# A planned order drawn up anew: other due times, and a longer landing time of scatter-adds in the table of costs

## Chip, core and metric

One core of a Trainium2 chip runs the whole kernel in one launch. The metric is the time of that launch in device microseconds (us). The engines are TensorE (PE, with its weight load PEld), VectorE (DVE), ScalarE (ACT), GpSimd (POOL) and SyncE (SP). SP issues most of the DMAs, ACT some of them, and POOL the indirect ones (gather and scatter).

## What is computed

The input x has the shape (32, 56, 56, 128): 32 images of 3136 tokens with 128 channels. Two layers follow each other.

```python
# layer 0
x = x + binary_conv3x3(LN(x))          # batch-norm over all images, then sign
t = t + moe(LN(t))                     # router, best 2 of 8 experts, each 128 -> 128
# layer 1
y = LN(x)
a = sigmoid((y @ Wa1) * (y @ Wa2)); b = sigmoid((y @ Wb1) * (y @ Wb2))
z = einsum("bikc,bkjc->bijc", a, b)    # 16 channels
x = x + sigmoid(y @ Wg) * (LN(z) @ Wz + bz)
t = t + ffn(LN(t))
def ffn(y):                            # each image by itself
    probs = softmax(y @ gate_w.T, axis=tokens)              # 64 experts
    vals, idx = top_k(probs, 8 tokens of each expert)
    pooled = sum over the 8 of vals * y[idx]                # one row per expert
    o = gelu(pooled @ W1 + b1) @ W2 + b2                    # 128 -> 512 -> 128
    out[idx] += vals * o                                    # scatter-add, 8 rows per expert
```

The last part matters most here: each image and each of the 64 experts give eight rows that are added to eight tokens of the output.

## The kernel before

**Tiles and stages.** The work is cut into 16 pairs of images, and each pair into 7 units of 896 tokens (a tile of 128 partitions x 7 x 128). A first pass over all 112 units gathers the statistics of the batch-norm (L494, L1843). Then the pairs flow through the stages: fetch and sign, convolution (L639) and its way back (L581), the mixture of experts (gate rows loaded by SP into gb, the product gb x xT on DVE in L833, the expert matmuls in L838, the sum in L850), the triangle mixing (L896, the z product in L982, L1095, L1117), and the logits of the 64 experts (L1168). In the steady state a pair comes out every 193 us, by the trace.

**The end of a pair.** `top8` searches the best eight tokens (L1195, L1199) on DVE, the softmax follows, and POOL gathers the tokens' rows with eight indirect DMAs (L1228). `pool_rows` adds them up weighted (L1246, L1248) and turns them on PE (tr_p, L1257).

**Late experts.** The 64 expert networks run in 16 groups of four. Each group runs twice, since its weights are needed for the images that are ready early and again for the last ones. `late_experts(False, g)` serves the first 13 pairs (images 0 to 25): weights on SP (L1418 the first, L1420 the second, L1465 the pooled rows, L1497 the bias), then ph (L1485), trh (L1509), gelu, po (L1531), and for each of the four experts a spreading product ps_eo (L1557), which lays an expert's output rows out for the eight tokens of every image. DVE scales them into a buffer eo (L1575, once for each of two lots: images 0 to 13, 112 rows, and 14 to 25, 96 rows), and POOL scatter-adds the buffer to the output (L1588). That makes 64 pairs of eo writes and 128 scatter-adds. There are four eo buffers (NEO, L73). Within a lot each scatter-add waits until the one before it has landed, since both may add to one token; between the lots POOL sets a byte in a memset (L1322), which keeps them apart. `late_experts(True, g)` ("alone") serves the last three pairs: its weights go to places of tiles that are done with (yT, the frames, lines, a_bd, gb, x, xT), the bias is added in L1517, and the results go to a buffer in memory (o_last_d, L1546).

**The last rows.** `last_sums` lays out for each of the last three pairs which expert adds to which token (store near_d in L1646, loads in L1650 and L1662, DVE in L1656, L1672 and L1680) and gathers the output rows concerned (L1696, 24 on POOL). `last_load` (L1721) brings the alone results back, in two parts: experts 0 to 47 and experts 48 to 63. `last_out_rows` multiplies (PE, L1744), adds (DVE, L1758), and POOL writes the rows out (L1775, 24 of them: 18 in the first part, 6 in the second).

**What sets the order.** Nothing is issued as the code is read. Each operation is recorded in an object of class `Order` (L92): engine, a duration in ns, for some a landing time, the tiles and keys that it reads and writes, and a rank. When all are recorded, `Order.run` (L166) plays the program through with these durations: on each engine it takes, of the operations that are ready, the one of lowest rank that can have its tiles; a tile comes free when its last user has ended. For a scatter-add that end is that of POOL plus the landing time:

```python
ends[k] = end + land
...
free[t.args[1]][slot[t]] = ends[k] + self.LAG[e]
```

The order found so is then emitted, and each engine keeps it on the chip whatever the real times are. The numbers in the table are costs for this planning only.

The rank is a due time in ticks. `TICK` (L38 to L69) has a row for each stage, with one number for each unit, batch, half or group; `PERIOD` is 14 ticks per pair:

```python
def at(p, tick):
    if tick > 19.3:
        tick = 19.3 + SHRINK.get(p, 1.0) * (tick - 19.3)
    return p * PERIOD + tick
```

`SHRINK` is 0.94 for the last pair. The 16 groups of `late_first` count from pair 13, those of `late_alone` and all rows of `last_` from pair 15. So a due time moves an operation on every engine that it uses, its SP and POOL issues too, as far as its inputs and buffers allow.

Of the kernel before, what the change touches and what calls it, by code (L numbers as in the profile page):

```python
# [35 lines left out]
PERIOD = 14  # L36

TICK = {  # L38
    "fetch": (-2.04, 1.47, 6.43, -9.37, 9.91, 4.03, 12.95),
    "sign": (0.13, 1.29, 1.62, 6.55, 7.92, 10.76, 8.15),  # L40
    "conv": (2.01, 2.39, 6.91, 8.17, 10.9, 11.53, 13.69),
    "conv_back": (3.38, 3.29, 7.78, 8.94, 11.21, 12.17, 14.95),
    "moe_turn": (6.33, 4.64, 9.97, 10.08, 12.86, 12.68, 15.65),
    "moe_gates": (6.55, 7.48, 10.31, 10.2, 14.16, 14, 16.57),
    "moe_experts": (10.08, 7.97, 10.43, 10.33, 15.78, 14.17, 16.99),
    "moe_add0": (10.49, 11.31, 14.68, 13.22, 16.78, 17.09, 19.52),
    "moe_add1": (10.74, 10.2, 14.52, 11.86, 17.39, 15.02, 19.11),
    "tri_turn": (16.98, 17.15, 20.55, 19.2, 19.88, 19.01, 20.48),
    "moe_stats": (4.49, 9.18, 12.45, 15.62),
    "moe_route": (6.46, 10.13, 12.89, 15.74),  # L50
    "tri_stats": (15.38, 15.09, 17.71, 20.29),
    "tri_b": (20.72, 21.13),
    "tri_a": (22.16, 21.48),
    "tri_z": (22.52,),
    "tri_out": (23.16, 22.58, 25.59, 25.25, 26.33, 28.87, 29.55),
    "gate_stats": (23.66, 26.32, 27, 31.44),
    "gate_turn": (25.56, 26.72, 27.08, 28.41, 30.53, 32.72, 31.77),
    "gate_logits": (26.34, 28.28, 30.27, 30.73, 30.88, 33.55, 33.56, 33.61),
    "clear": (33.78,),
    "top8": (36.48,),  # L60
    "pool_rows": (40.09,),
    "late_first": (28.35, 29.89, 30.07, 31.23, 36.99, 38.58, 41.48, 41.79, 42.49, 44.88, 49.22,
        50.09, 53.49, 56.47, 57.12, 73.25),
    "late_alone": (48.05, 52.09, 68.6, 70.4, 66.27, 52.32, 44.78, 60.5, 76.55, 41.92, 67.99,
        67.49, 84.16, 107, 76.56, 68.5),
    "last_sums": (54.98, 70.08, 51.49),
    "last_load": (79.71, 120.93),
    "last_rows": (102.26, 131.4, 121.75, 140.19, 135, 143.81),
}  # L69

AHEAD_CHAIN = 2
# [214 lines left out]
def kernel(ctx: ExitStack, tc: tile.TileContext, a: dict, out: bass.AP):  # L286
# [116 lines left out]
    def apart(ins, k):  # L403

        for other in range(len(LOTS)):
            if other != k:
                tc.declare_no_dep(ins, group=f"lot{other}", reason="the lots' tokens differ")
        tc.add_to_no_dep_group(f"lot{k}", ins)


    with ExitStack() as c2:
# [32 lines left out]
        def new(tag, shape, name, dtype=F32):  # L444
            return op.tile(pools.get(tag, work), tag, shape, dtype, name)
# [4 lines left out]
        def bank(name):  # L450
            return new("ps", [128, 512], name)
# [867 lines left out]
        def part_lots(lot):  # L1319

            if pool_lot["last"] not in (None, lot):
                nc.gpsimd.memset(between, 0.0)  # L1322
            pool_lot["last"] = lot
# [33 lines left out]
        def late_experts(alone, g):  # L1357
# [74 lines left out]
            for j in range(NE):  # L1432
                h = homes[j]
                if h == "p":
                    for k, of in ((0, first_w), (1, second_w)):
                        _, key, (keys, base) = of[j]

                        @op("SP", 360, r=[open_place(keys, base)], w=[key], land=868)
                        def _(j=j, k=k):
                            load_w(j, k)  # L1440
                elif h == "g" and alone:
                    @op("SP", 720, w=[first_w[j][1]], land=1736)
                    def _(j=j):
                        load_w(j, 0)
                        load_w(j, 1)
                else:
                    @op("SP", 360, w=[first_w[j][1]], land=868)
                    def _(j=j):
                        load_w(j, 0)

                    if alone:
                        load_second(j)
# [9 lines left out]
            else:  # L1462
# [17 lines left out]
            @op(  # L1480
                "PE", 1000, r=[key for _, key, _ in first_w] + [(side1, "t")], w=[ph, ("ph", name)]
            )
            def _():
                for j in range(NE):
                    nc.tensor.matmul(  # L1485
                        ph.ap[32 * j : 32 * j + 32, :], lhsT=tok()[:, j].rearrange("c p i -> c (p i)"),
                        rhs=first_w[j][0](),
                        start=True, stop=True,
                    )
# [37 lines left out]
            @op("PE", 1100, r=[hG] + [key for _, key, _ in second_w], w=[po])  # L1527
            def _():
                for k in range(HID4):
                    for j in range(NE):  # L1530
                        nc.tensor.matmul(  # L1531
                            po.ap[32 * j : 32 * j + 32, :C],
                            lhsT=hG.ap[:, k, 32 * j : 32 * j + 32], rhs=second_w[j][0]()[:, k * C : (k + 1) * C],
                            start=(k == 0), stop=(k == HID4 - 1),
                        )
# [14 lines left out]
            for j in () if alone else range(NE):  # L1550
                ps_e = bank(f"ps_eo_{name}_{j}")

                @op("PE", 2 * 222, r=[(side2, "o")], w=[ps_e])
                def _(q=B * j, ps_e=ps_e):
                    for k, (i0, i1) in enumerate(LOTS[:2]):
                        rows = (i1 - i0) * K1
                        nc.tensor.matmul(  # L1557
                            ps_e.ap[:rows, k * C : (k + 1) * C],
                            lhsT=spread[q : q + B, k, :rows], rhs=side2.ap[q : q + B, 5, :],
                            start=True, stop=True,  # L1560
                        )

                eo = new("eo", [128, 2, C], f"eo_{name}_{j}")

                for lot in range(2):
                    i0, i1 = LOTS[lot]
                    rows = (i1 - i0) * K1
                    e = g * NE + j

                    @op(  # L1570
                        "DVE", 230, r=[ps_e] + [("picked", p) for p in range(i0 // 2, i1 // 2)],
                        w=[(eo, lot)],
                    )
                    def _(eo=eo, lot=lot, rows=rows, e=e, ps_e=ps_e, k=lot):
                        nc.vector.tensor_scalar(  # L1575
                            eo.ap[:rows, lot, :], ps_e.ap[:rows, k * C : (k + 1) * C],
                            gains[lot][:rows, e : e + 1], None, ALU.mult,
                        )

                    @op(  # L1580
                        "POOL", 2000, land=4200,
                        r=[(eo, lot)] + [("out", p, u) for p in range(i0 // 2, i1 // 2)
                                         for u in range(NU)][: None if e == 0 else 0],
                        w=[("lot", lot)],
                    )
                    def _(eo=eo, lot=lot, rows=rows, e=e):
                        part_lots(lot)
                        ins = nc.gpsimd.indirect_dma_start(  # L1588
                            out=tokens_out,
                            out_offset=bass.IndirectOffsetOnAxis(  # L1590
                                ap=picked[lot][:rows, e : e + 1], axis=0
                            ),
                            in_=eo.ap[:rows, lot, :], in_offset=None, compute_op=ALU.add,
                        ).ins

                        for before_ in last_out.get(lot, stored[lot]):
                            tc.add_manual_dep(ins, before_, sync, reason="adds to the same tokens")
                        apart(ins, lot)
                        last_out[lot] = [ins.name]
# [598 lines left out]
```

## Time and profile before

| what | value |
|---|---|
| time, median of 3 runs | 3759.09 us (3744.3 to 3762.89) |
| time of the profiled execution | 3770.89 us |
| its span; mean granted clock of TensorE | 3769.1 us; 0.958 |
| PE busy / PEld busy | 3440.6 us (91%) / 2811.6 us (75%) |
| DVE / ACT / POOL busy | 3223.4 (86%) / 2371.0 (63%) / 464.6 us (12%) |
| DMA | 834.19 MB, 221 GB/s in the mean |
| first and last eo write (L1575) | 3180.3 and 3664.9 us |
| first and last scatter-add issued (L1588) | 3180.9 and 3688.7 us; 128, mean 1693 ns of POOL each |
| search of the last pair (L1195); its first and last gather (L1228) | 3604.09; 3613.99 and 3622.85 us |
| first issue of the last rows (L1775) | 3724.2 us |

The profile is of one execution. A share of busy time is a mean over the whole span, and the busy tenths by slices (40 slices of 94 us) show that the run has two halves of unequal kind:

```profile
PE   7998899999999999999999999999999999897654
DVE  8996789898989898999999898889898989786561
POOL 0000000101010101010101000010101011625554
PEclk9999999999999999999999999999999999998766
```

Each digit is the busy share of a slice in tenths. For 33 slices PE is at 9 nearly throughout, and DVE at 8 to 9. In the last six slices POOL has its work, and PE and DVE fall off.

### The profile page before, as it was taken

The page shows a single profiled execution, that of the slowest core. Times are in us where ns is not written, and L with a number is a line of the kernel's source. Part 1 is how long each engine was busy: PE and PEld are TensorE (multiplying, and loading weights), DVE is VectorE, ACT ScalarE, POOL GpSimd, SP SyncE. Part 2 cuts the span into 40 slices and gives each one's busy share as a digit, 9 for nine tenths or more (in the row PEclk, how much of TensorE's full clock was granted, in tenths as well). Part 3 has the DMA queues.
Part 4 walks back from the last instruction along what each step waited for, and adds up shares of the span by engine and source line. Part 5 has one row for each costly group of instructions (what it writes and reads, how often), then busy time and mean ns, then how long its engine had stood idle before and what let it go on. Part 6 is the DMA issues. An engine that isn't in the chain of part 4 may idle for free.

```text
span 3769.1 us, 79927 instructions
## 1 busy us (share of the span) xinstructions
PE 3440.6 (91%) x28307; PEld 2811.6 (75%) x28307; DVE 3223.4 (86%) x10730; ACT 2371.0 (63%) x5436; POOL 464.6 (12%) x526
## 2 busy tenths in 40 slices
PE   7998899999999999999999999999999999897654
PEld 7886787777778787878787878777777778676432
DVE  8996789898989898999999898889898989786561
ACT  6997446757575848484848485757575766655431
POOL 0000000101010101010101000010101011625554
PEclk9999999999999999999999999999999999998766
DMA  8995546666565656565656666656474747788785
GB/s 305 361 356 219 200 178 209 214 200 218 199 223 186 227 191 223 196 227 192 221 204 216 207 219 205 221 185 244 165 250 164 263 150 264 227 268 249 179 258 169
DMA packets 340849, 834.19 MB, mean 221 GB/s; under 512 B 87249, under 2 KB 115874, under 8 KB 340450
## 3 DMA queue, kind: packets, MB, share of 16 engines
q1 hardware_dynamic: 281378, 711.14, 54.5%
q10 hardware_dynamic: 38080, 99.57, 6.8%
q0 software_dynamic: 20992, 18.37, 3.0%
q8 instruction: 225, 3.69, 0.4%
q14 instruction: 174, 1.43, 0.1%
HBM read 654.71 MB, written 174.18 MB: 220 GB/s over the span
## 4 chain that ended last, share of the span: by engine, by line
PE 49%; DVE 34%; DMA 8%; issue 5%; ACT 3%; POOL 1%; another core or an unknown queue 0%; ACTq 0%; SPq 0%; POOLq 0%; DVEq 0%
PE acc L838 22%; DVE gb L833 8%; PE ps_cv L639 6%; DVE stln L494 5%; PE gram L1843 4%; DMA gb<-gate 4%; PE tr L483 3%; DMA out<-eo_False,picked 2%; DVE sg L1108 2%; DVE x L1117 2%; DVE x L581 2%; PE trc L483 2%; DVE frame L617 2%; PE ps_b L896 2%; PE ps_z L982 1%
## 5 line engine op out<-in xcount | busy, mean ns | idle before, releaser
L838 PE MATMUL acc<-expert_w,gb 128*128 128x128 f32 x12544 | 1488.0, 278 | 67.1 <-DVE gb L833 55.4
L838 PEld LDWEIGHTS acc<-expert_w,gb 128*128 128x128 f32 x12544 | 1439.3, 193 | 137.6 <-DVE gb L833 52.7
L833 DVE TENSOR_TENSOR gb<-gb,xT 128x1024 f32<-128x1024 f32 x784 | 947.0, 1220 | 41.2 <-DMA gb<-gate 38.8
L494 DVE BATCH_NORM_STATS2 stln<-x 128x6 f32<-128x128 f32 x2352 | 569.9, 288 | 2.5
L639 PE MATMUL ps_cv<-frame,w_sign 128*128 128x448 bf16 x2016 | 418.2, 356 | 8.8 <-DVE frame L617 8.3
L568 ACT ACTIVATE yl<-x,rmln 128x128 f32<-128x128 f32 x756 | 320.0, 491 | 97.7 <-DVE rmln L553 82.2
L568 ACT ACTIVATE yt<-x,rmln 128x128 f32<-128x128 f32 x784 | 326.2, 489 | 49.6 <-DVE rmln L556 33.3
L568 ACT ACTIVATE ym<-x,rmln 128x128 f32<-128x128 f32 x784 | 326.4, 494 | 30.1 <-DVE rmln L556 29.2
L639 PEld LDWEIGHTS <-w_sign 128*128 128x128 bf16 x2016 | 196.2, 98 | 182.8 <-issue 17.3
L647 ACT ACTIVATE cv<-ps_cv,cv_shift,cv_scale 128x448 f32<-128x448 f32 x224 | 161.3, 722 | 154.8 <-PE ps_cv L639 144.6
L1083 ACT ACTIVATE sg<-ps_g 128x512 f32<-128x512 f32 x224 | 115.2, 537 | 224.7 <-PE ps_g L1073 219.8
L1124 POOL MEMSET a_bd<- 128x2048 f32 x15 | 27.6, 1841 | 1824.9 <-PE ps_zo L1095 1707.7
L1588 POOL DMA_INDIRECT out<-eo_False,picked x128 | 216.7, 1693 | 235.7 <-DVE eo_False L1575 119.6
L1228 POOL DMA_INDIRECT rows<-y,near x128 | 132.3, 1034 | 864.1 <-PE trt L483 760.0
L568 ACT ACTIVATE y<-x,rm 128x128 f32<-128x128 f32 x448 | 211.5, 725 | 11.7 <-DVE rm L553 11.5
L1073 PE MATMUL ps_g<-wg,yT 128*128 128x128 f32 x1568 | 203.4, 279 | 8.6 <-DVE eo_False L1575 5.5
L850 DVE TENSOR_TENSOR x<-acc,x 128x512 f32<-128x512 f32 (+1 forms) x224 | 139.9, 625 | 74.3 <-PE acc L838 73.6
L581 DVE TENSOR_TENSOR x<-trc,x 128x512 f32<-128x512 f32 (+1 forms) x224 | 132.6, 619 | 81.5 <-PE trc L483 80.1
L1073 PEld LDWEIGHTS ps_g<-wg,yT 128*128 128x128 f32 x1568 | 188.5, 194 | 13.2 <-DVE eo_False L1575 5.7
L1843 PE MATMUL gram<-y 128*128 128x128 f32 x1568 | 196.0, 278 | 0.3 <-DVE y L572 0.3
L494 DVE BATCH_NORM_STATS2 st<-x 128x6 f32<-128x128 f32 x784 | 187.5, 284 | 6.4 <-DMA x<-in_x 6.4
L1843 PEld LDWEIGHTS gram<-y 128*128 128x128 f32 x1568 | 192.2, 198 | 1.0 <-DVE y L572 0.5
(266 smaller groups left out, 5515.7 us busy)
## 6 DMA issues: line engine op xcount, KB each, us to landing
gb<-gate SPq DMA_DIRECT2D x784, 512.0 KB
x<-in_x SPq DMA_DIRECT2D x224, 448.0 KB
y<-yT SPq DMA_DIRECT2D x112, 448.0 KB
ys<-y SPq DMA_DIRECT2D x112, 448.0 KB
out<-x ACTq DMA_DIRECT2D x105, 448.0 KB
y<-yl ACTq DMA_DIRECT2D x105, 448.0 KB
w_False<-in_L_ffn_weight SPq DMA_DIRECT2D x128, 256.0 KB
w_True<-in_L_ffn_weight SPq DMA_DIRECT2D x102, 256.0 KB
```

What stands on the lines that cost most here:

```text
L483: nc.tensor.transpose(ps.ap[:, n * 128 : (n + 1) * 128], get()[:, n0 + n, :], ident)
L494: nc.vector.bn_stats(st.ap[:, c0 + k, :], src.ap[:, k, :])
L568: nc.scalar.activation(dst.ap[:, k, :], src.ap[:, k, :], AF.Identity, bias=m, scale=r)
L581: nc.vector.tensor_tensor(xf, ps.ap[:, : k * 128], xf, ALU.add)
L639: nc.tensor.matmul(acc, lhsT=w_sign[:, tap, :], rhs=frames[f][:, 8 * band + kh : 8 * band + kh + 8, kw : kw + W], start=(tap == 0), stop=( ...
L647: nc.scalar.activation(cv.ap[:, :, 64 * h : 64 * h + 64], ps.ap[:, :448].rearrange("c (q n) -> c n q", n=N7), AF.Identity, bias=cv_shift, ...
L833: nc.vector.tensor_tensor(gb.ap, gb.ap, over(xT.ap[:, n, :], E0), ALU.mult)
L838: nc.tensor.matmul(acc.ap[:, n % 4 * C : (n % 4 + 1) * C], lhsT=gb.ap[:, e, :], rhs=expert_w[:, e * C : (e + 1) * C], start=(e == 0), stop ...
L850: nc.vector.tensor_tensor(dst, acc.ap[:, : k * C], dst, ALU.add)
L1073: nc.tensor.matmul(psg.ap[:, n * C : (n + 1) * C], lhsT=yT[:, n0 + n, 16 * u : 16 * u + 16, :].rearrange("c r v -> c (r v)"), rhs=wg, star ...
L1588: ins = nc.gpsimd.indirect_dma_start(out=tokens_out, out_offset=bass.IndirectOffsetOnAxis(ap=picked[lot][:rows, e : e + 1], axis=0), in_=e ...
L1843: nc.tensor.matmul(gram.ap[:, :C], lhsT=y.ap[:, n, :], rhs=y.ap[:, n, :], start=(g % G16 == 0 and n == 0), stop=(g % G16 == G16 - 1 and n ...
```

## The change

All 28 rows of `TICK` get new numbers, and the scatter-add is entered with 1900 instead of 2000 ns of POOL and with 6000 instead of 4200 ns to land. No operation is added, removed or altered; only the order in which the engines get them is planned anew. The diff, cut to the rows of which the text speaks:

```diff
 TICK = {
-    "fetch": (-2.04, 1.47, 6.43, -9.37, 9.91, 4.03, 12.95),
+    "fetch": (-1.33, 2, 7.43, -3.54, 10.29, 1.66, 11.46),
...
-    "moe_experts": (10.08, 7.97, 10.43, 10.33, 15.78, 14.17, 16.99),
+    "moe_experts": (10.1, 7.94, 10.43, 10.35, 15.91, 13.95, 18.28),
...
-    "tri_z": (22.52,),
+    "tri_z": (22.47,),
...
-    "top8": (36.48,),
-    "pool_rows": (40.09,),
-    "late_first": (28.35, 29.89, 30.07, 31.23, 36.99, 38.58, 41.48, 41.79, 42.49, 44.88, 49.22,
-        50.09, 53.49, 56.47, 57.12, 73.25),
-    "late_alone": (48.05, 52.09, 68.6, 70.4, 66.27, 52.32, 44.78, 60.5, 76.55, 41.92, 67.99,
-        67.49, 84.16, 107, 76.56, 68.5),
-    "last_sums": (54.98, 70.08, 51.49),
-    "last_load": (79.71, 120.93),
-    "last_rows": (102.26, 131.4, 121.75, 140.19, 135, 143.81),
+    "top8": (38.16,),
+    "pool_rows": (40.16,),
+    "late_first": (28.07, 31.48, 31.51, 32.94, 36.66, 38.56, 39.84, 41.94, 42.64, 46.08, 46.48,
+        53.47, 54.13, 58.24, 59.75, 78.8),
+    "late_alone": (52.38, 58.66, 71.37, 72.8, 68.05, 51.14, 45.65, 56.43, 78.56, 47.51, 57.97,
+        69.44, 82.18, 110.61, 83.12, 68.58),
+    "last_sums": (54.22, 60.23, 49.3),
+    "last_load": (80.05, 117.28),
+    "last_rows": (109.25, 138.58, 140.44, 162.06, 163.8, 140.66),
 }
...
                     @op(
-                        "POOL", 2000, land=4200,
+                        "POOL", 1900, land=6000,
                         r=[(eo, lot)] + [("out", p, u) for p in range(i0 // 2, i1 // 2)
                                          for u in range(NU)][: None if e == 0 else 0],
                         w=[("lot", lot)],
```

More of the change, by code (lines that the diff above doesn't have):

```diff
@@ L38 @@
 TICK = {
-    "fetch": (-2.04, 1.47, 6.43, -9.37, 9.91, 4.03, 12.95),
[L40 to L44, printed above, removed]
-    "moe_experts": (10.08, 7.97, 10.43, 10.33, 15.78, 14.17, 16.99),
-    "moe_add0": (10.49, 11.31, 14.68, 13.22, 16.78, 17.09, 19.52),
@@ L47 @@
[L47 to L53, printed above, removed]
-    "tri_z": (22.52,),
-    "tri_out": (23.16, 22.58, 25.59, 25.25, 26.33, 28.87, 29.55),
-    "gate_stats": (23.66, 26.32, 27, 31.44),
-    "gate_turn": (25.56, 26.72, 27.08, 28.41, 30.53, 32.72, 31.77),
@@ L58 @@
-    "gate_logits": (26.34, 28.28, 30.27, 30.73, 30.88, 33.55, 33.56, 33.61),
-    "clear": (33.78,),
-    "top8": (36.48,),
-    "pool_rows": (40.09,),
-    "late_first": (28.35, 29.89, 30.07, 31.23, 36.99, 38.58, 41.48, 41.79, 42.49, 44.88, 49.22,
-        50.09, 53.49, 56.47, 57.12, 73.25),
-    "late_alone": (48.05, 52.09, 68.6, 70.4, 66.27, 52.32, 44.78, 60.5, 76.55, 41.92, 67.99,
-        67.49, 84.16, 107, 76.56, 68.5),
-    "last_sums": (54.98, 70.08, 51.49),
-    "last_load": (79.71, 120.93),
@@ L68 @@
-    "last_rows": (102.26, 131.4, 121.75, 140.19, 135, 143.81),
+    "fetch": (-1.33, 2, 7.43, -3.54, 10.29, 1.66, 11.46),
+    "sign": (-0.27, 1.66, 1.97, 7.44, 7.57, 10.48, 8.32),
+    "conv": (2.26, 2.5, 7.48, 7.92, 11.01, 11.54, 13.42),
+    "conv_back": (3.69, 3.17, 7.67, 9, 11.26, 12.29, 15.6),
+    "moe_turn": (6.41, 4.55, 9.24, 10.15, 12.9, 13.35, 16),
+    "moe_gates": (6.77, 7, 10.27, 10.35, 14.3, 13.46, 16.22),
+    "moe_experts": (10.1, 7.94, 10.43, 10.35, 15.91, 13.95, 18.28),
+    "moe_add0": (10.33, 12.45, 12.23, 15.12, 16.48, 14.77, 19.48),
@@ new lines @@
+    "moe_add1": (13.72, 9.22, 13.19, 10.93, 16.42, 17.24, 19.13),
+    "tri_turn": (17.62, 17.71, 20.47, 19.34, 19.57, 19.86, 20.75),
+    "moe_stats": (4.13, 9.09, 12.35, 15.92),
+    "moe_route": (6.43, 10.15, 13.35, 16.12),
+    "tri_stats": (15.07, 15.6, 17.58, 19.82),
+    "tri_b": (21.08, 21.54),
+    "tri_a": (22.11, 21.55),
+    "tri_z": (22.47,),
+    "tri_out": (23.62, 22.63, 25.71, 25.44, 26.37, 29.11, 29.68),
+    "gate_stats": (23.84, 25.96, 27.37, 31.14),
+    "gate_turn": (25.6, 26.93, 27.69, 28.4, 30.17, 32.68, 31.72),
@@ new lines @@
+    "gate_logits": (26.55, 28.52, 30.46, 31.35, 30.79, 33.46, 34.22, 34.02),
+    "clear": (32.85,),
+    "top8": (38.16,),
[6 more added lines that the diff above has]
+    "last_load": (80.05, 117.28),
```

## The prediction

> **What bounds the kernel now.** I read the page first, then windows by stage, then the chain of waits where the windows thin out, then what VectorE (DVE) waits for there, and last GpSimd (POOL) in order of time.
>
> The windows (columns: length, then PE, PEld, DVE, ACT, POOL busy, granted clock, DMA share, GB/s) divide the run into two parts.
>
> ```profile
> 800.00:2800.00 2000.00, 1914.88 (x15587) 1573.27 (x15587) 1812.09 (x5704) 1310.83 (x2904) 118.81 (x101) 0.99 0.60 209
> ...
> 3180.00:3380.00 200.00, 181.51 (x1630) 146.59 (x1623) 165.71 (x528) 126.26 (x262) 90.47 (x97) 0.97 0.83 254
> 3380.00:3480.00 100.00, 79.91 (x745) 66.71 (x748) 73.38 (x214) 56.59 (x121) 57.15 (x56) 0.88 0.83 247
> 3480.00:3640.00 160.00, 97.91 (x833) 62.35 (x833) 87.67 (x326) 71.96 (x125) 88.18 (x111) 0.72 0.76 213
> 3640.00:3769.00 129.00, 60.37 (x692) 32.03 (x691) 44.57 (x129) 16.26 (x28) 67.54 (x103) 0.71 0.64 195
> ```
>
> Up to about 3180 us the kernel is bound by TensorE (1914.88 of 2000 us busy), with DVE close behind (1812.09). The scatter-adds begin at 3180.9 us. From there PE falls to 80 of 100 us and then to 98 of 160: only this tail can hold a gain of any size. In the stretch of 100 us the chain reads:
>
> ```profile
> by line: DMA out<-eo_False,picked 62.2%; PE acc L838 8.5%; DVE eo_False L1575 6.3%; issue 5.7%; DVE m L1195 3.9%; DVE gb L833 2.4%; PE ps_g L1073 1.6%; PE ps_eo_False L1557 1.5%; PE po_False L1531 1.2%; PE trh_False L1509 0.8%; POOL between
> ...
> 3405.25 9.22 DMA out<-eo_False,picked
> 3414.60 0.62 DVE eo_False L1575 x2
> 3415.25 5.77 DMA out<-eo_False,picked
> 3421.11 0.62 DVE eo_False L1575 x2
> 3421.78 5.27 DMA out<-eo_False,picked
> ```
>
> That is 62.2% of 85 us (asked from 3385 to 3470): 52.9 us in which the chain hangs on the landing of a scatter-add, 5.3 to 9.2 us each from issue to release. L1575 writes one of four eo buffers and must wait until the scatter-add of four pairs earlier has landed. DVE is in order, so the expert products (L833), the statistics and everything else stand behind it. What DVE itself waited for from 3380 to 3480 us (sum, times, longest):
>
> ```profile
> DVE eo_False L1575 <- DMA out<-eo_False,picked: 21.7, 8, 5.0
> DVE lg L755 <- PE ps_r L725: 1.4, 1, 1.4
> ```
>
> So 21.7 us of 26.6 idle. After 3480 us other things are late: the last pair's chain of dependent steps, then, from 3631 us on, the weights of the 16 groups "alone". The end is a row of L1775 on POOL, 1.28 us apart:
>
> ```profile
> 3693.07 0.95 POOL L1696 DMA_INDIRECT rows_last<-out,at_last  x1 [0.30 <-issue]
> 3724.16 0.99 POOL L1775 DMA_INDIRECT out<-rows_last,at_last  x1 [30.06 <-DVE rows_last L1758]
> ```
>
> POOL stands idle for 30 us there: the scatter-adds, the last of them at 3688.73, are not what the end waits for.
>
> **The change, part by part.** All sums are made against the profiled execution: span 3769.1, its own time 3770.89, which is 11.8 above the median of 3759.09. No instruction is added or taken out but a few of POOL's separating memsets (531 to 528 instructions). Two numbers change in the planner, 28 rows of due times are new, and what moves is order.
>
> (a) *The first 3100 us.* I compared the two built orders place by place. The first pass over x is the same. From pair 2 to pair 12 the z product of each pair (L982) and its top-8 search (L1195) stand at the same place of their engines, and about 3% of PE's places hold another line, all swaps of near neighbours (units 4 and 5 exchanged, one L838 group past one transpose). In between, where the first two pairs start (480 to 800 us), order differs in a quarter to a third of PE's places, but the last L838 of pair 0 has 3.7 us more PE work ahead of it, its z product none. PE is busy 304.64 of 320 us there, so at most 15 us could be won. Bounds for all of this: -8 to +8 us, the ends being half of those 15 us and one swap losing 0.7 us in each of 12 periods. I take 0: the nearest rows, the waits of L838 for gb, are 35.8 us over 2300 us and nothing in the order shortens or lengthens them as a whole.
>
> (b) *Where the eo writes stand.* I added up DVE's work ahead of each pair of eo writes, each instruction at the mean of its line in the trace. There are 64 pairs, one per expert; four make a group. Work ahead, before and after, in us:
>
> ```
> pair        8       24      28      32      36      39      48      52      56      63
> before   3442.4  3598.4  3611.1  3638.7  3656.7  3680.9  3697.2  3743.0  3750.4  3797.4
> after    3455.0  3595.6  3618.2  3640.6  3673.7  3681.7  3723.7  3748.1  3770.8  3813.7
> ```
>
> From pair 24 to 36 the old order gives DVE (3656.7 - 3598.4)/12 = 4.9 us of work per pair. The chip took (3467.42 - 3394.94)/10 = 7.25 us per pair (POOL's issues of pairs 24 and 34). The shortfall is 12 x 2.35 = 28 us; the trace shows 21.7 us of waits, so the four buffers absorb some 6. The new order gives (3673.7 - 3595.6)/12 = 6.5 us per pair: shortfall 12 x 0.75 = 9, less 6 is 3. The eight gathers of pair 14 (L1228, 1.28 us each) now stand between pairs 31 and 33 instead of after 34; each pair leaves about 3.7 us of POOL's time free (7.25 - 2 x 1.76), so of 10.2 us some 3 remain. Waits left: 6; waits gone: 21.7 - 6 = 16. Pairs 36 to 39 are then packed into 8 us of work, but at a place where DVE is half idle (3480 to 3640: 87.67 of 160). Bounds of the gain: 0, if something else is late at once, to 21.7. PE is next: it must make up the same work, and it had only 20 us idle in that stretch. I take two thirds of 16: -11. From 3180 to 3380 DVE's own eo waits are 5.9 us (4.6 and 1.3); groups 1 and 2 move 11 to 13 us of work later. Bounds 0 to -5.9; I take -2.
>
> [...] The row says 5.3 to 9.2 us under a DMA share of 0.83, so I keep 7.25. [...]
>
> (c) *The last pair's gathers.* Before, POOL issued one scatter-add between the search result (3611.70) and the first gather (3613.99); in the new order none stands there: -1.8. Four pairs more (52 to 55) stand behind the eight gathers.
>
> (d) *SP's queue.* The second weights of group 15 (four L1420, L1497) now stand behind the first near_d store (L1646), which waits for pair 15's softmax (DVE, 3615.2). Before they left from about 3612.3. So they leave 4 us later. They feed po_False 15, which stands ahead of tr_p 15 on PE, and with that ahead of all "alone" groups; but tr_p (3630.14) had to wait for gathers issued up to 3622.85 anyway. Bounds 0 to +4; with (c) I take +2 for both.
>
> (e) *POOL's chain at the end.* Behind the last gather of L1228 (3622.85) stand 12 pairs, before 8.5. Before, 17 issues of L1588 ran from 3624.10 to 3688.73, with gathers of L1696 among them: 64.6/8 = 8.1 us per pair. Twelve pairs then end at 3623 + 12 x 8.1 = 3720. L1775 first issues at 3724, so 4 us are left; and its last six issues start at 3755.43 after another 8.5 us of idle POOL, which would take up a late start. So nothing moves until a pair takes over (3724 + 8.5 - 3623)/12 = 9.1 us; from there every us per pair costs 12. Cost 0. The loads for the alone groups queue the same set ahead of near_d, so the bytes left after it are the same.
>
> Sum: 0 - 11 - 2 + 2 + 0 = -11. Span 3758, own time 3760; moved to the median, 3759 - 11 = 3748.
>
> **Rivals.** (1) *Likeliest, 3748 (3740 to 3758), chance 0.38*: the sum above. For it: one wait holds 21.7 us and the order loosens exactly it. (2) *All of it comes, 3726 (3712 to 3740), 0.30*: the 21.7 and 5.9 us go, and PE, granted 0.88 instead of 0.99 of its clock in that stretch, gets up to 0.1 x 80 = 8 us back; 3759 - 28 - 5 = 3726. Against it: the shortfall of 0.75 us per pair remains. (3) *Hidden anyway, 3759 (3758 to 3766), 0.10*: the alone weights set the end. DMA share is 0.94 to 1.03 in most of 3660 to 3720, and an earlier start only fills queues that are full. Against: its share is 0.43 to 0.68 from 3500 to 3560. (4) *Slower, 3777 (3766 to 3795), 0.22*: the scatter-adds become the end. The scatter-adds of one lot follow one another: each waits until its forerunner has landed. With the longest landing of the chain above, 9.2 us, and the shortest L1588, 1.4 us, a pair takes 10.6 us, over the 9.1 of (e), and L1775 is late by 12 x 1.5 = 18 us: 3759 + 18 = 3777. Besides, the last eo write of group 15 needs pair 59 landed (3623 + 8 x 10.6 = 3708), where DVE came to that place at 3702.5 before, and stops the bias adds (L1517) behind it for 5 us, beside the first delay. For it: the share of DMA is 0.94 to 1.03 there. Against: before, with nearly that share, a pair took 8.1.
>
> **How the numbers follow.** About 0.5% (19 us) is what a measurement of this kernel can tell from no change. Below 3740: all of (2) and a little of (1): 0.32. Above 3778: half of (4), and 0.07 taken from (1) for swaps of (a) that cost more than their bound: 0.18. Between: 0.50. The range leaves out the outer third of (2) and of (4): 3716 to 3788.
>
> **What would show it.** Right: L1575's wait for the scatter-add between 3380 and 3480 us falls from 21.7 to about 6, PE there rises from 80 to about 88, pair 15's top-8 search (3604.09) starts some 11 us earlier, and POOL is still idle ahead of L1775. (2) shows in a search before 3585; (3) in an early search with an unchanged end; (4) in L1775 following straight on L1588, or in L1575 waits past 3640. If the first eo write (3180.3) moves by over 5 us, (a) was wrong.

## The result, and the profile after

The changed kernel takes 3727.5 us (median of 9 runs, 3718.8 to 3732.6), the kernel before 3752.3 (9 runs, 3743.2 to 3762.9): a ratio of 0.9927, 95% interval 0.9913 to 0.9940, or 27 us less (the medians differ by 25). The profiled execution took 3728.7 us with a span of 3726.8. The profile of before, at 3770.9 us, was of an execution 18.6 above its median, so the two profiles lie 42 us apart. That has to be kept in mind with every difference below.

First the milestones. Each is the start of an instruction in the trace: L982 of a pair for its z product, L1195 of the last pair for the last search.

| stretch, us | before | after | difference |
|---|---|---|---|
| start to the z product of pair 2 | 936.0 | 929.2 | -6.8 |
| from there to the z product of pair 13 (11 pairs) | 2133.0 | 2111.0 | -22.0 |
| from there to the last search | 535.1 | 533.7 | -1.4 |
| last search to the end | 165.0 | 152.9 | -12.1 |

The prediction set the first two rows at 0 and looked for all of the gain in the third. The second row is the surprise: two us in every pair of a steady state whose PE order is nearly the same. The fourth will turn out not to belong to the change.

The windows after. The second line here is the stretch that answers to 3380 to 3480 of before, moved by the 35 us by which the work around it came earlier.

```profile
3180.00:3380.00 200.00, 182.82 (x1680) 144.69 (x1681) 168.53 (x546) 129.89 (x268) 89.19 (x98) 0.96 0.83 253
3345.00:3445.00 100.00, 84.25 (x761) 67.02 (x753) 71.89 (x220) 63.27 (x136) 49.47 (x53) 0.90 0.88 269
...
3480.00:3640.00 160.00, 104.16 (x898) 66.37 (x898) 102.56 (x353) 59.99 (x100) 81.71 (x103) 0.70 0.80 239
3640.00:3726.00 86.00, 37.17 (x464) 21.88 (x460) 17.52 (x61) 11.00 (x19) 48.91 (x79) 0.69 0.62 182
```

In that stretch PE rose from 80 to 84 us, not to 88. What DVE waited for there (sum, times, longest):

```profile
DVE x L850 <- PE acc L838: 8.2, 4, 4.2
DVE eo_False L1575 <- DMA out<-eo_False,picked: 7.5, 2, 6.1
DVE acc L1248 <- DMA rows<-y,near: 4.9, 3, 2.6
```

The wait for scatter-adds fell from 21.7 to 7.5 us, close to the 6 predicted, and two other waits now stand beside it. In the chain of waits from 3350 to 3435 us a landing scatter-add holds 27.5%, where it held 62.2%. Last, POOL at the end:

```profile
3687.55 1.41 POOL L1588 DMA_INDIRECT out<-eo_False,picked  x1 [0.99 <-DMA out<-eo_False,picked]
...
3690.43 1.01 POOL L1775 DMA_INDIRECT out<-rows_last,at_last  x1 [1.43 <-DVE rows_last L1758]
```

The 30 us of idle POOL ahead of L1775 are gone: the last rows follow on the last scatter-add after 1.4 us. Twelve pairs took 8.0 us each ((3687.55 - 3591.1)/12), as step (e) had it, and the cover is used up, but not exceeded.

### The profile page after: what moved, and what is told of

It is laid out like the page before. It is cut to its first block, busy times and chain, and to the rows that moved or that the text cites. A ratio compares the mean times of both kernels' runs of the same rounds, so it can differ in the third digit from the quotient of the medians.

```text
span 3726.8 us, 79886 instructions
## 1 busy us (share of the span) xinstructions
PE 3423.5 (92%) x28307; PEld 2801.9 (75%) x28307; DVE 3212.2 (86%) x10730; ACT 2369.1 (64%) x5440; POOL 454.8 (12%) x523
## 4 chain that ended last, share of the span: by engine, by line
PE 50%; DVE 32%; DMA 10%; issue 3%; ACT 3%; POOL 1%; SPq 0%; ACTq 0%; DVEq 0%; POOLq 0%
PE acc L838 22%; DVE gb L833 8%; PE ps_cv L639 6%; DVE stln L494 5%; DMA gb<-gate 4%; PE gram L1843 4%; PE tr L483 3%; DVE sg L1108 2%; DMA w_True<-in_L_ffn_weight 2%; DVE x L581 2%; DVE x L1117 2%; PE ps_z L982 1%; PE ps_l L1168 1%; PE trc L483 1%; DVE frame L617 1%
## 5 line engine op out<-in xcount | busy, mean ns | idle before, releaser
L568 ACT ACTIVATE yl<-x,rmln 128x128 f32<-128x128 f32 x756 | 319.5, 489 | 89.3 <-DVE rmln L553 65.2
L568 ACT ACTIVATE ym<-x,rmln 128x128 f32<-128x128 f32 x784 | 327.3, 492 | 48.5 <-DVE rmln L556 46.6
L568 ACT ACTIVATE yt<-x,rmln 128x128 f32<-128x128 f32 x784 | 326.7, 487 | 43.6 <-DVE rmln L556 33.3
L1588 POOL DMA_INDIRECT out<-eo_False,picked x128 | 203.0, 1586 | 250.3 <-DVE eo_False L1575 115.1
L568 ACT ACTIVATE y<-x,rm 128x128 f32<-128x128 f32 x448 | 210.1, 714 | 11.6 <-DVE rm L553 10.1
```

What stands on the lines that cost most here:

```text
L568: nc.scalar.activation(dst.ap[:, k, :], src.ap[:, k, :], AF.Identity, bias=m, scale=r)
L1588: ins = nc.gpsimd.indirect_dma_start(out=tokens_out, out_offset=bass.IndirectOffsetOnAxis(ap=picked[lot][:rows, e : e + 1], axis=0), in_=e ...
```

## Where two us of each pair come from

The steady part first, from the z product of pair 2 to that of pair 13 (columns as in the windows above). Before:

```profile
936.00:3069.00 2133.00, 2042.85 (x16635) 1682.43 (x16634) 1932.41 (x6040) 1393.82 (x3080) 128.66 (x110) 0.98 0.60 208
```

After:

```profile
929.20:3040.20 2111.00, 2021.20 (x16634) 1670.04 (x16633) 1921.92 (x6040) 1389.19 (x3080) 129.54 (x110) 0.99 0.60 211
```

The same instructions take 22 us less of PE, 10.5 less of DVE, and the granted clock is a little higher (0.99 against 0.98). Lay PE's instructions of each pair over those of the same pair in the other kernel, counted from the pair's z product. Over most of a pair they drift by up to some 3 us, in either direction. At one place all eleven pairs move the same way: between 158 and 178 us after the z product each gains 0.7 to 3.0 us, 19.5 of the 22 us in sum. Shortly before it, in pair 8, DVE looks like this before the change (start, us, engine, line):

```profile
2258.69 0.15 DVE L1218 RECIPROCAL sq<-sq 128x1 f32<-128x1 f32 x1
2258.87 2.27 DVE L1219 TENSOR_SCALAR pg<-pg,sq 128x8 f32<-128x8 f32 x1
2259.01 2.13 DVE L526 SCALAR_TENSOR_TENSOR rmln<-q_ln,rmln 128x7 f32<-128x7 f32 x1
2259.09 2.06 DVE L746 TENSOR_TENSOR k<-k,mk 128x112 f32<-128x112 f32 x1
2261.19 0.17 DVE L552 TENSOR_TENSOR q_ln<-stln 128x7 f32<-128x7 f32 x1
```

and POOL, before, over the same time:

```profile
2258.57 0.94 POOL L1228 DMA_INDIRECT rows<-y,near  x1 [0.30 <-issue]
2259.50 1.62 POOL L1045 MEMSET zv<- 128x1792 f32 x1
2261.28 0.95 POOL L1228 DMA_INDIRECT rows<-y,near  x1 [0.16 <-issue]
```

L1219 multiplies eight numbers in each partition. It takes 0.23 us in the last three pairs and 2.27 here, and it ends, with the two instructions behind it, within 0.03 us of the end of the memset of zv on POOL (2259.50 + 1.62 = 2261.12). After, on DVE:

```profile
2242.91 0.16 DVE L1218 RECIPROCAL sq<-sq 128x1 f32<-128x1 f32 x1
2243.10 1.04 DVE L1219 TENSOR_SCALAR pg<-pg,sq 128x8 f32<-128x8 f32 x1
2243.24 0.90 DVE L526 SCALAR_TENSOR_TENSOR rmln<-q_ln,rmln 128x7 f32<-128x7 f32 x1
```

and on POOL:

```profile
2241.56 0.95 POOL L1228 DMA_INDIRECT rows<-y,near  x1 [0.30 <-ACT lgT L1212]
2242.51 1.60 POOL L1045 MEMSET zv<- 128x1792 f32 x1
2244.27 0.95 POOL L1228 DMA_INDIRECT rows<-y,near  x1 [0.16 <-issue]
```

The new order has put the memset one gather earlier: behind the third of the pair's eight gathers instead of the fourth, 1.25 us. L1219 meets its second half only. Over pairs 1 to 12 L1219 took 2.27 to 2.28 us before and 1.03 to 1.04 after.

The traces show the stall, not its mechanism. Not every instruction on DVE is held: L1218, a reciprocal, runs in 0.16 us inside the memset after the change (from 2242.91 us, the memset from 2242.51). One thing does not fit a hold that begins with the memset's record: before, L1219 starts 0.63 us ahead of the recorded start and, at 0.23 us, should have been through by then. The gather that runs at that moment is not what holds it, as the kernel with the memset behind the eighth gather shows below. Either the hold begins before the memset's record or that record starts late; no run here tells which.

What becomes of the 1.24 us is seen on PE (trt, trc and trg are transposes). Before:

```profile
2262.61 1.49 PE L483 MATMUL trt<-ident,yt 128*128 128x128 f32 x4 [0.30 <-ACT yt L568]
2266.94 0.63 PE L803 MATMUL trg<-ident,gg 128*56 128x128 f32 x2 [2.84 <-DVE stln L494]
2267.36 1.06 PE L483 MATMUL trc<-ident,cv 128*128 128x128 f32 x4
...
2269.63 2.54 PE L896 MATMUL ps_b<-yT,wb 128*32 128x448 f32 x22
```

After:

```profile
2246.39 0.69 PE L483 MATMUL trt<-ident,yt 128*128 128x128 f32 x4
2249.96 0.41 PE L803 MATMUL trg<-ident,gg 128*56 128x128 f32 x2 [2.88 <-DVE gg L789]
2250.20 0.60 PE L483 MATMUL trc<-ident,cv 128*128 128x128 f32 x4
...
2251.39 3.21 PE L896 MATMUL ps_b<-yT,wb 128*32 128x448 f32 x28
```

The instructions stuck behind L1219 finish the last units' statistics and gates, and PE comes to trt and trg just then. Counted from the start of L1219, trg begins at 8.07 us before and 6.86 after: 1.21 us, the stall itself. It is not in the wait right ahead of trg, which is the same in both (2.84 and 2.88 us). It lies one step earlier, in trt, whose inputs come from ScalarE (L568), which waits for DVE's L556 behind the stall (0.72 us before, 0.17 after): before, trt starts after 0.30 us of idle time and takes 1.49 us, after it 0.69. The kernel before_m3 of the next section has the order of before, but for the memset; over its eleven pairs trt takes 75.8 us of PE where before took 83.8, the idle time ahead of trt falls from 5.3 to 0.5 us, and that ahead of trg stays (35.7 and 35.8).

L896 begins at 10.76 and 8.29 us: another 1.26 us. These come from the clock: before, four transposes of trc take 1.06 us at a granted clock of 0.50, after it 0.60 us at 1.00. By the record of the granted clock TensorE ran at half of it for 64.9 us within these eleven pairs before and for 41.0 after; a stretch of it begins some 6 to 9 us after the start of L1219 in all eleven pairs before and in nine of them after. If work at half the clock takes twice as long, as the transposes nearly do, (64.9 - 41.0)/2 = 12 us of the 22 are lost so; the stall on the way accounts for the rest (11 x 1.24 is 13.6 at most).

The bare gap ahead of trg is the same with either order (2.84 and 2.88 us) and does not tell the two apart. What differs in the trace is the stretch around it: from the end of trc to trg PE does four transposes in 4.6 us before (2262.31 to 2266.94); after, they follow trc without a gap, and PE then does nothing for 2.9 us. Which of this moves the clock is not shown.

## Experiments

The kernels ran on three chips, each with the kernel before beside it on the same chip. The medians of before were 3752.7, 3768.9 and 3750.8 us, so ratios to before are compared. A ratio and a difference of medians can lie a few us apart. For the result above the chip is not on record. Each profile, here too, is of one execution. Theory A puts the gain on the memset; theory B, the prediction's, on the waits for scatter-adds. P and Q are two answers to what such a wait is worth: two thirds of it (P), or next to nothing, since something else is late at once (Q). None of the kernels leaves work out.

### The memset alone

In three kernels only POOL's order is altered. After planning, the memset of pair p+1 is put behind a given gather of pair p:

```diff
+        for one, other in self.moves:
+            out.remove(one)
+            out.insert(out.index(other) + 1, one)
...
+        for p in range(1, 12):
+            op.moves.append((op.marks["clear", p + 1], op.marks["gather", p, 2]))
```

The third index (2: the third gather) is 3 and 7 in the other two.

> The order of before, with one thing altered: in pairs 1 to 11 POOL's memset of zv (L1045 before) goes behind the third gather of top8 (L1228) and no longer behind the fourth; all other engines keep their order. Theory A (the memset holds VectorE's L1219 for 2.3 us instead of 1.0, the last units' gates come later, TensorE waits for them and drops to half its clock): L1219 falls from 2.27 to about 1.04 us, the pair period from 193.9 to about 191.9, the time by 11 x 2.0 = 22 us or somewhat less, to 3728 to 3738. Theory B (the gain is all in the tail, where scatter-adds held the eo writes, as predicted): no change, 3752 within 5.

> The changed order, with the memset of zv put back behind the fourth gather in pairs 1 to 11. Theory A: L1219 takes 2.27 us again, the pair period goes from 191.9 to about 193.9, the time from 3727.5 to 3742 to 3750. Theory B: no change, 3727 within 5.

> The changed order, with the memset of zv moved behind the eighth gather in pairs 1 to 11, 5 us later, where L1219 is over. Theory A: L1219 falls from 1.04 to 0.23 us, the period from 191.9 to some 190.5 to 191, the time from 3727.5 to 3710 to 3720, unless the memset then holds another VectorE instruction of that kind. Theory B: no change, 3727 within 5.

Before with the memset behind the third gather: 3731.9 us, ratio 0.9950 (0.9937 to 0.9964). The changed kernel with it behind the fourth: 3743.1, ratio 0.9981 (0.9968 to 0.9994). Behind the eighth: 3717.7, ratio 0.9904 (0.9890 to 0.9917). L1219 (it is L1229 in these; min, median, max in ns) in the first:

```profile
L1229 DVE TENSOR_SCALAR pg<-pg,sq x16: 230/1030/2278, 709.3 to 3586.2; 128x8 f32<-128x8 f32 x16
```

in the second:

```profile
L1229 DVE TENSOR_SCALAR pg<-pg,sq x16: 230/2278/2279, 702.5 to 3599.1; 128x8 f32<-128x8 f32 x16
```

and in the third:

```profile
L1229 DVE TENSOR_SCALAR pg<-pg,sq x16: 230/231/1475, 705.5 to 3580.3; 128x8 f32<-128x8 f32 x16
```

In the third, a gather on POOL starts 0.3 us ahead of this instruction, as it does in before (2258.57 there), runs until after its end and does not hold it. Pair 8, DVE and POOL:

```profile
2240.53 0.23 DVE L1229 TENSOR_SCALAR pg<-pg,sq 128x8 f32<-128x8 f32 x1
```

```profile
2240.22 0.95 POOL L1238 DMA_INDIRECT rows<-y,near  x1 [0.30 <-ACT yT L868]
```

The duration follows the memset, in either order of everything else, and so do the times. One POOL instruction moved by one place makes before 0.5% faster, 19 us (0.36 to 0.63%, 14 to 24); put back, it takes 0.54% (0.9981 - 0.9927) from the changed kernel, 20 us (13 to 27). By the medians these are 21 and 16 us. Theory A holds, and theory B's "no change" falls in both. Pair period and half clock over all profiles of the study, by place of the memset:

| memset behind gather | kernels | us per pair (pairs 2 to 12) | us at half clock in 11 pairs |
|---|---|---|---|
| 4 | before, after_m4, before_eo5, before_eo3, land_only | 193.5 to 194.0 | 55 to 65 |
| 3 | after, after_again, before_m3, front_new, front_6000, after_eo5 | 191.5 to 192.0 | 14 to 41 |
| 8 | after_m8, after_m8_again, after_m8_eo5 | 191.2 to 192.0 | 20 to 48 |

The first two rows do not overlap. The third does not show what I expected of it: L1219 loses its last 0.8 us, but the pair period stays. Whether the memset holds another DVE instruction in its place, no figure here shows. The time of that kernel is lower all the same, and was so on another chip, beside the changed kernel itself:

> The changed kernel once more, as the measure for the three beside it. A ratio to before of 0.991 to 0.994, as in its first runs, if the gain does not depend on the chip; 0.996 or more if it does.

> The changed order with the memset of zv behind the eighth gather in pairs 1 to 11, as before on another chip. Theory A: 6 to 12 us under the changed kernel beside it. If the 10 us were the chip's: within 3 us of it.

They took 3725.0 (ratio 0.9930, 0.9910 to 0.9950) and 3718.8 us (0.9908, 0.9887 to 0.9928). So 6 to 10 us less by the medians, with intervals that overlap. Its two profiles are of executions of 3725.0 and 3731.0 us, above its medians, and don't show where it gains.

### The waits for scatter-adds, with nothing moved

Here the planner plans with four eo buffers, and the kernel has five or three: no engine's order changes, only how long an eo write waits. With five, the sums of the first pass lie in the tile yT, to make room.

```diff
-                    t.make(self.slots[t.args[1]])
+                    t.make({"eo": 5}.get(t.args[1], self.slots[t.args[1]]))
```

> Before, every engine in the same order, but five real eo buffers for four (the sums of the first pass lie in yT meanwhile, to make room). It takes away part of L1575's waits for scatter-adds without moving anything. In before's trace they are 32.4 us after 3040 us; each burst can spare one pair, some 7 us, so 12 to 18 should be left. Theory P (as predicted, two thirds of such a wait are gained): 10 to 13 us faster, 3740 to 3743. Theory Q (another engine is late at once, the wait is hidden): 0 to 4 us faster, 3749 to 3753.

> Before, every engine in the same order, but three real eo buffers for four. It adds waits for scatter-adds: some 7 us in each of the four to six bursts, 32 to 60 or 70 us. Theory P: two thirds of the 30 to 40 us added come out at the end, 3770 to 3780. Theory Q: less than a third, 3752 to 3764.

> The changed kernel with five real eo buffers for four, order unaltered. Its waits for scatter-adds are 21.8 us; 5 to 12 should be left. Theory P: 7 to 11 us faster, 3717 to 3721. Theory Q: 0 to 3 us faster, 3725 to 3728.

> The same with five real eo buffers for four, every engine's order unaltered. It takes away what is left of the waits for scatter-adds, some 18 us. Theory P (two thirds of them are gained): 10 to 12 us under the kernel with four. Theory Q (other waits take their place at once): within 4 us of it.

With five buffers in before, the wait fell from 32.4 to 11.3 us, and the time by 0.14% (0.02 to 0.27%): 5 us (1 to 10) for 21 us of wait (11.3 from its own profile, 32.4 from that of before). In its profile pair 2's z product comes 2 to 4 us later than in the two other kernels with before's front on that chip (941.1 against 936.8 and 939.0 us), so the move of the sums may hide a little of the gain. With three it rose to 91.3 us, and what is put down to issue on the same line from 4.6 to 14.5; the time rose by 1.33% (1.11 to 1.54%), 50 us for 69. With five in the changed kernel no wait for a scatter-add is left in the trace, and with the memset behind the eighth gather the time is 3716.8 (ratio 0.9910, 0.9891 to 0.9928) against 3718.8 with four on the same chip: no gain that six runs of each can tell from none, for 18.9 us of wait. So theory Q holds for what is taken away, P for what is added. The changed kernel with five buffers gave 3760.0 on the chip where before took 3768.9 (0.9980, 0.9966 to 0.9994), which neither theory expected. Its trace keeps the gain of the front (pair 13's z product at 3036.5 us, where before with five buffers had it at 3069.6 on that chip), and from the last search to the end it took 171.8 us, against 164.9. But that execution took 3742.0 us, the fastest of the twelve, so it does not show where the median loses another 18. The changed kernel did not run on that chip, so whether it would have lost the same there is open.

What takes the place of such a wait is seen in two executions on one chip, from pair 13's z product to the last search. Before's order with the memset moved (535.4 us):

```profile
DVE eo_False L1587 <- DMA out<-eo_False,picked: 29.8, 11, 4.9
DVE x L858 <- PE acc L846: 15.7, 8, 3.9
DVE sg L1118 <- PE ps_zo L1105: 13.5, 3, 11.4
...
DVE abm_b L937 <- ACT abm_b L932: 5.4, 2, 4.0
```

The new order with the memset put back (531.1 us):

```profile
DVE x L858 <- PE acc L846: 15.5, 6, 5.5
DVE sg L1118 <- ACT sg L1093: 14.9, 2, 14.7
DVE abm_b L937 <- ACT abm_b L932: 12.4, 3, 7.9
DVE w_False L1551 <- PE po_False L1543: 11.1, 3, 5.1
DVE acc L1260 <- DMA rows<-y,near: 10.5, 7, 4.1
DVE m L1205 <- ACT lgT L1187: 7.8, 3, 5.1
DVE gb L841 <- DMA gb<-gate: 6.9, 11, 1.1
```

The scatter-adds' 29.8 us are down to 3.0. But all waits of DVE there sum to 116.5 us in the first and 117.6 in the second: ScalarE's gate and mixing (L1093, L932), the gathers and the gate rows hold it instead. The stretch is 4.3 us shorter. Other profiles agree: five of the new order with four eo buffers have 526.8 to 533.7 us there, the two of the old one 535.1 and 535.4. In all, the changed kernel is 0.23% (9 us, some 2 to 16) below before with the memset moved by the ratios, and 4 us by the medians; some 3 of it lie in the start (929.2 against 932.2 us to pair 2).

### The halves of the change

> The new due times in the rows from fetch to pool_rows only; the late_ and last_ rows and the scatter-add (2000 ns, 4200 ns to land) as before. Theory A: the first 12 pairs run as in the changed kernel (period 191.9 us) and the tail as before: most of the 25 us come, 3728 to 3738. Theory B: none of it comes, 3747 to 3757, and L1575 still waits some 22 us for scatter-adds in the stretch after pair 14's search.

> Before's due times with the scatter-add entered at 1900 and 6000 ns. The front is the same to the 12th pair, memset behind the fourth gather included. The planner spreads the eo writes, so their waits should fall from 32 to 15 to 22 us as in the changed kernel. Theory A (the gain is in the front): 3745 to 3755. Theory B (the gain is the eo waits): 3730 to 3742.

> The new due times from fetch to pool_rows, the scatter-add entered at 1900 and 6000 ns, the late_ and last_ rows as before. With the late rows as before and 4200 ns the tail took 714.8 us from pair 13's z product to the end, in the changed kernel 686.6. If the landing time alone mends it: within 8 us of the changed kernel. If the rows must be drawn for it: 20 us or more above the changed kernel, as the old table with 6000 ns was 36 above before.

The edits are the rows named, and in land_only this line alone:

```diff
-                        "POOL", 2000, land=4200,
+                        "POOL", 1900, land=6000,
```

| kernel | median, us | ratio (95%) | pair 2 to 13 | pair 13 to last search | search to end | scatter waits |
|---|---|---|---|---|---|---|
| front_new | 3756.2 | 1.0008 (0.9996 to 1.0020) | 2108.6 | 561.9 | 152.9 | 52.3 |
| front_6000 | 3747.9 | 0.9988 (0.9977 to 1.0000) | 2107.9 | 559.0 | 154.8 | 32.2 |
| land_only | 3800.3 | 1.0097 (1.0075 to 1.0120) | 2129.4 | 556.6 | 174.9 | 26.2 |
| before_m3 | 3731.9 | 0.9950 (0.9937 to 0.9964) | 2107.7 | 535.4 | 152.8 | 31.8 |
| after | 3727.5 | 0.9927 (0.9913 to 0.9940) | 2111.0 | 533.7 | 152.9 | 21.8 |

My expectation of front_new fell. The front's gain is there to the full, and 26 to 28 us are lost again behind pair 13, since the late rows were drawn for the old front. The landing time alone doesn't mend it (front_6000), and put into the old table it costs 0.97%. land_only has fewer scatter waits than before and is slower by 36 us (by the medians 31): in this tail the length of that one wait says little about the time. So the late rows, drawn anew, are worth some 23 us by the medians of one chip (3747.9 against 3725.0), but as what the new front needs, not as a gain over before.

The column "search to end" clears up the fourth row of the first table: before's own tail order takes 152.8 us in before_m3. The 165 in the profile of before are thus not its order's. They go with the chip: the four profiles from the chip where before took 3768.9 us have 164.9 to 174.9 there (land_only is one of them), all nine others after this one 152.8 to 158.1. Why the chips differ is not shown. What sets this stretch after the change is seen in the chain of waits from 3480 us on:

```profile
3612.01 6.96 DMA w_True<-in_L_ffn_weight
3631.19 8.41 DMA w_True<-in_L_ffn_weight
3639.66 8.12 DMA w_True<-in_L_ffn_weight
3661.58 6.92 DMA w_True<-in_L_ffn_weight
```

These loads, the weights of the groups "alone", hold 28.8% of it.

## Why the prediction was right, and where it was wrong

The time lies in the stated range and on the predicted side. It fell by 25 to 27 us, where the likeliest case had 11 and rival 2 had 33, at 3726. But rival 2's mechanism is not what happened: some 20 us come from the memset, a cause that no step of the prediction has, so that the time fell where it was looked for is luck. Rival 2's sign came too, a search before 3585 (it began at 3573.9), yet 28.8 of its 30.1 us were won ahead of pair 13's z product. Of the signs of being right, the wait fell as foreseen, PE rose half as far, and POOL was not idle ahead of L1775.

**Step (a) failed.** It said 0 for the first 3100 us, bounded at 8, from the places of two lines (L982 and L1195) and of PE's instructions. That comparison left POOL out, where the memset stands one gather earlier, as the order itself shows. And it took the durations of before for granted: with those, POOL's order costs nothing as long as POOL is idle (it was busy for 119 of 2000 us). The runs put 19 us there by before_m3 and 20 by after_m4, where the step had 0. Its last sentence of the section on signs named the symptom: the first eo write moved by 30.5 us (3180.3 to 3149.8). The start gained 6.8 us, in its bounds.

**Step (b) was right about the wait and wrong about its worth.** The wait fell from 21.7 to 7.5 us in its stretch (6 predicted). Two thirds of what is taken away was to be gained; before_eo5 measured about a quarter (5 of 21 us), after_m8_eo5 nothing. "PE is next" was named as the risk; what came next were ScalarE and the gathers. After the change, too, scatter-adds hold the chain for 5.76 to 9.77 us each there, from the start of the issue to the release, where step (b) had read 5.3 to 9.2.

**Step (c)** had -1.8 us from search to first gather: 9.9 became 8.3. **Step (d)**'s delay doesn't show: from the search to tr_p 26.0 us became 21.4. **Step (e)** had 8.1 us per pair and no cost: 8.0, and none. Rival 4 added L1588's 1.4 us to a landing of 9.2 that was counted from the start of the issue, and so held POOL's part (6.29 us there) already. Its sign, L1775 straight behind L1588, came without its loss, since the chain ends in the alone weights (rival 3's mechanism, for this last stretch).

The best version run is the changed order with the memset behind the eighth gather: 0.9904 and 0.9908 of before, against 0.9927 and 0.9930 of the change.

## What to carry to other kernels

When only an order changes, compare every engine's order, the idle ones too: here an instruction on an engine that is busy 6% of the time (POOL, 119 of 2000 us) lengthened one on DVE from 0.23 to 2.27 us, and its move by one place was worth 19 to 20 us. A duration that varies for one line (231 to 2274 ns) is the row that says so. The longest wait of a bound engine is not what its removal is worth; lengthen and shorten it alone, with the order held, before counting on it. A planner's due times fit one another: half of a new table was worth nothing here, and its new landing time alone cost 1%.

## What the runs showed of the hardware

A tensor_scalar of 0.23 us on VectorE took 2.27 us, to the end of a 1.6 us memset on GpSimd that began, by the record, 0.63 us after it. Beside a gather alone it took 0.23. A stall of 1.24 us on VectorE cost TensorE 2.47 us in pair 8 and, by the 19 to 20 us of the experiments, about 1.8 in the mean, as more time at half clock followed it (64.9 us before, 41.0 after, in eleven pairs).
